# Moving x, sums and reciprocal transfers one step later in the first ten strips of an attention layer

## The chip, the cores and the metric

The kernel runs on one core of a Trainium2 chip. The metric is the device time of one execution in microseconds; the median of several executions is compared. The engines are TensorE (PE; its weight loads are shown as PEld), VectorE (DVE), ScalarE (ACT) and GpSimd (POOL). SyncE (SP) issues most of the transfers between the memory on the chip and HBM; GpSimd issues the indirect ones.

## The reference

The input x is 2 x 256 x 56 x 56. Two layers follow, each a mixer and a mixture of experts (MoE), both with a residual. Cut to its steps, with the weights left out:

```python
# layer 0: attention over a 7x7 window, 8 heads of 32, then 8 experts, the best two
x = x + attention(ln_c(x))              # q, k, v, o are 256x256; softmax over 49 neighbours
t = to_tokens(x)                        # 6272 tokens of 256
t = t + moe0(ln_t(t))                   # moe0(u) = u + sum over two experts of
x = from_tokens(t)                      #   weight * (gelu(u @ w1[e] + b1[e]) @ w2[e] + b2[e])
# layer 1: two ternary 3x3 convolutions with batch normalization, then 8 experts
x = x + conv(ln_c(x))                   # relu(o1 + bn(conv3x3(o1))), o1 = relu(bn(conv3x3(x)))
t = to_tokens(x)
t = t + moe1(ln_t(t))                   # hidden 512, the two largest probabilities as weights
```

The change lies in layer 0, between the attention's sums and the rows that are handed to the experts.

## The kernel before

**Strips.** The image is cut into 14 strips of 8 rows by 56 columns, seven to each of the two images. A strip has 448 tokens, held as four tiles of 112. The attention loop (L1577 to L1599) has one iteration for each strip g, and an iteration has eight steps: four column tiles by two halves of the channels. A step writes `scores` of its tile (q times k, L1435 and L1444, and the exponential, L1454) and `attend` of the step before: `av` on PE (L1464), added into `acc` by VectorE (L1474). `av` has two buffers. `acc` holds, for each pair of heads, the weighted values and, in further partitions, the sums of the exponentials. A step then advances `project(g + 2)` (the layer norm and q, k, v of a later strip) and calls `push`, which takes one step of every generator in `under_way`; a `yield` in such a generator therefore stands for one step of the loop.

**Leaving.** A strip can be finished once the strip below it has been attended to, as the windows overlap. So `leave(g - 1)` joins `under_way` at the end of iteration g; the last strip of an image follows with four steps' delay. `leave` (L1478 to L1548) does this:

- it loads x again and adds the output bias (`again`, L1319 and L1320);
- it writes the sums of the exponentials from `acc` to HBM (`sums`, L1491) and reads them back in another layout (`den`, L1496);
- it takes the reciprocal on VectorE (L1499), writes it to HBM (`shares`, L1500) and reads it back to the partitions of the heads (`rec`, two transfers, L1503); three small operations, `fit`, check the range of the sums (L1509 to L1511);
- it multiplies `acc` by `rec` into `oc` (eight operations of VectorE, L1520); for the first image `fresh` (L1354) then sets the strip's rows of `acc` for the second one;
- it multiplies by the output weights (`pw`, L1533) and adds to x (L1541);
- `norm0` normalizes the tokens (statistics on VectorE, the power on POOL at L713 to L715, the scaling on ScalarE at L721), transposes them (`pu`, L763; `ut`, L768), adds u to x on POOL (L770), stores x (`x_mid`, L771) and forms the gate's logits (`pl`, L777; the copy, L788). For strips 12 and 13 VectorE does what POOL does for the others.

For each pair of strips `settle0` then chooses two experts a token (L804 to L820, VectorE), ranks the rows (`rk` on PE) and scatters each row twice to its expert's place in HBM (16 indirect transfers of POOL, L860).

**The experts of layer 0.** The first 27 tiles of 128 rows or more are planned with the rows of the first ten strips alone (`FIRST`, L66): the plan is there when `counted0` is set by strip 9 (L832). In before the loop after the attention (L1601) pushes until the plan exists; by then it does. The remaining steps of `leave` and `settle0` for the last strips are taken one for each expert tile (`beside`), and when they are through, `routed_all` plans the later tiles. A tile has a load of its rows (`xg`, L1038), of its weights (`w`, L1049), transposes (`pt`, L1059), two products (`ph`, L1091; `py`, L1108) and a scatter of the result (L1118).

**Order.** Every engine, and every queue of transfers, executes in order what it has been given. An instruction that waits for a semaphore holds all behind it on its engine; for a transfer issued by SP that means all later transfers of SP. In the attention the order within each engine is set when the kernel is built, by a scheduler that works on the instructions as they are written down, so it doesn't always equal the written order. In the experts it is written out by hand for SP, VectorE, PE and ScalarE. Tile pools give out buffers in turn: `sums`, `shares`, `den` and `rden` have two each, `rec`, `oc` and `ut` one.

Of the kernel before, what the change touches and what calls it, by code (L numbers as in the profile page):

```python
# [10 lines left out]
F32 = mybir.dt.float32  # L11
# [4 lines left out]
ALU = mybir.AluOpType  # L16
# [22 lines left out]
LEAST, MOST = 1e-15, 1e15  # L39

E = 8
TT = NQ
# [22 lines left out]
DEN = HEADS * NT // TT  # L65
FIRST = (10, 10)  # L66
# [10 lines left out]
def bcast(ap, axis, shape):  # L77
    return ap.unsqueeze(axis).to_broadcast(shape)
# [551 lines left out]
def metaformer(ctx: ExitStack, tc: tile.TileContext, a: dict, out: bass.AP, flag):  # L630
    nc = tc.nc
# [87 lines left out]
    def scaled(dest, src, rstd, nmr):  # L719
        for t in range(NTT):  # L720
            nc.scalar.activation(  # L721
                dest[:, t, :],
                src[:, t, :],
                AF.Identity,
                bias=nmr[:, t : t + 1],
                scale=rstd[:, t : t + 1],
            )

    def routing(layer, wp, tp, ps):
# [18 lines left out]
        def norm(i, src, late=False):  # L748


            eng = nc.vector if late else small_eng
            rstd, nmr = yield from token_stats(tp, src, eps5, layer == 1 or late)
            row = rows[i] = tp.tile([TT, NTT, RW], F32, tag="u", name="u", bufs=U_BUFS[layer])
            u = row[:, :, :C]
            eng.memset(row[:, :, R_EX + 1 :], 0.0)
            eng.tensor_copy(row[:, :, R_ID], ids[:, i * NTT : (i + 1) * NTT])
            scaled(u, src, rstd, nmr)
            yield
            ut = tp.tile([P, KC, NT], F32, tag="ut", name="ut", bufs=1)
            for k in range(KC):  # L760
                pu = ps.tile([P, 512], F32, tag="aux", name="pu")
                for t in range(NTT):
                    nc.tensor.transpose(  # L763
                        pu[:, t * TT : (t + 1) * TT],
                        u[:, t, k * P : (k + 1) * P],
                        ident[:TT, :TT],
                    )
                nc.scalar.copy(ut[:, k, :], pu[:, :NT])  # L768
            if layer == 0:
                eng.tensor_tensor(src, src, u, ALU.add)  # L770
                nc.sync.dma_start(x_mid[i], src)  # L771
                yield
            lg = lgs[:, i * NTT : (i + 1) * NTT, :]
            pl = ps.tile([TT, NTT, E], F32, tag="pl" if layer else "aux", name="pl")
            for t in range(NTT):
                for k in range(KC):
                    nc.tensor.matmul(  # L777
                        pl[:, t, :],
                        ut[:, k, t * TT : (t + 1) * TT],
                        gate[:, k, :],  # L780
                        start=k == 0,
                        stop=k == KC - 1,
                    )
            if layer == 1:
                yield
                nc.vector.tensor_tensor(lg, pl, bcast(gate_b, 1, [TT, NTT, E]), ALU.add)
            else:
                nc.vector.tensor_copy(lg, pl)  # L788
            yield
# [400 lines left out]
    def blocks(ap):  # L1190

        return ap.rearrange("p h (t w) -> p t h w", w=TW)
# [100 lines left out]
    with ExitStack() as st:  # L1293
        aw = st.enter_context(tc.tile_pool(name="att_w", bufs=1, reuse_waits="tile"))
        tp = st.enter_context(tc.tile_pool(name="att_t", bufs=2, reuse_waits="tile"))
        ps = st.enter_context(tc.tile_pool(name="att_ps", bufs=2, space=PSUM, reuse_waits="tile"))
# [47 lines left out]
        fits = aw.tile([TT, DEN], F32, tag="fits", name="fits")  # L1344
# [15 lines left out]
            nc.gpsimd.memset(t[:, :, :, 1:3, :], 1.0)  # L1360
            vals.append(t)
        keys = {}
        norm0, settle0, tiles0, gates0, wgt0, counted0, _ = routing(0, aw, tp, ps)

        def project(g):
            s = g % NS
# [111 lines left out]
        def leave(g):  # L1478

            s = g % NS  # L1480
            rows = slice(s * SR, (s + 1) * SR)

            late = g >= len(STRIPS) - 2
            again(g, nc.vector if late else nc.gpsimd)


            sums = dram.tile([2, PAIRS * NT], F32, tag="sums", name="sums", bufs=2)
            shares = dram.tile([2, PAIRS * NT], F32, tag="shares", name="shares", bufs=2)
            den = tp.tile([TT, DEN], F32, tag="den", name="den")
            rden = tp.tile([TT, DEN], F32, tag="rden", name="rden")  # L1490
            for i in range(2):  # L1491
                nc.sync.dma_start(
                    sums[i : i + 1, :].rearrange("i (j h w) -> i j h w", h=SR, w=W),
                    acc[HD * (i + 1) : HD * (i + 1) + 1, :, rows, :],
                )
            nc.sync.dma_start(den, sums.rearrange("i (p n) -> (i p) n", n=DEN))  # L1496
            yield
            yield
            nc.vector.reciprocal(rden, den)  # L1499
            nc.sync.dma_start(shares.rearrange("i (p n) -> (i p) n", n=DEN), rden)  # L1500
            rec = tp.tile([P, PAIRS, NT], F32, tag="taken", name="rec", bufs=1)
            for i in range(2):
                nc.sync.dma_start(  # L1503
                    rec[3 * HD * i : 3 * HD * i + HD].rearrange("p j n -> p (j n)"),
                    shares[i].partition_broadcast(HD),
                )

            fit = tp.tile([TT, DEN], F32, tag="fit", name="fit")
            nc.vector.tensor_scalar(fit, den, LEAST, None, ALU.is_ge)  # L1509
            nc.vector.scalar_tensor_tensor(fit, den, MOST, fit, ALU.is_le, ALU.mult)  # L1510
            nc.vector.tensor_tensor(fits, fits, fit, ALU.add)  # L1511
            yield
            yield
            oc = tp.tile([P, KC, NT], F32, tag="oc", name="oc", bufs=1)
            for i in range(2):
                at = slice(3 * HD * i, 3 * HD * i + HD)
                for j in range(2):
                    to = HD * (2 * j + i)
                    for k in range(KC):
                        nc.vector.tensor_tensor(  # L1520
                            oc[to : to + HD, k, :].rearrange("p (t h w) -> p t h w", h=SR, w=TW),
                            blocks(acc[at, 2 * k + j, rows, :]),
                            blocks(rec[at, 2 * k + j, :].rearrange("p (h w) -> p h w", w=W)),
                            ALU.mult,
                        )
            if g < NS:
                fresh(s)
            yield
            for t in range(0, NTT, 2):
                pw = ps.tile([TT, 2, C], F32, tag="aux", name="pw")  # L1530
                for i in range(2):
                    for k in range(KC):
                        nc.tensor.matmul(  # L1533
                            pw[:, i, :],
                            oc[:, k, (t + i) * TT : (t + i + 1) * TT],
                            wt["o"][:, k, :],
                            start=k == 0,
                            stop=k == KC - 1,
                        )
                x = xr[g][:, t : t + 2, :]  # L1540
                nc.vector.tensor_tensor(x, pw, x, ALU.add)  # L1541
            yield
            yield from norm0(g, xr.pop(g), late)
            routed.append(g)
            if late:
                under_way.append(settle0([g]))
            elif g ^ 1 in routed:
                under_way.append(settle0([g & ~1, g | 1]))  # L1548
# [8 lines left out]
        def push():  # L1557

            for it in under_way[:]:
                if next(it, it) is it:  # L1560
                    under_way.remove(it)

        plans0, taken = [], []
# [34 lines left out]
                before = None  # L1598
                under_way.append(later(4, leave(g)))  # L1599
        loop.close()  # L1600
        while not plans0:  # L1601
            push()
            plan_first()

# [77 lines left out]
    with mid:  # L1682

        with ExitStack() as st:
            rp = st.enter_context(tc.tile_pool(name="raw", bufs=1, reuse_waits="tile"))
            tp = st.enter_context(tc.tile_pool(name="conv_t", bufs=2, reuse_waits="tile"))
            ps = st.enter_context(tc.tile_pool(name="conv_ps", bufs=4, space=PSUM, reuse_waits="tile"))
# [128 lines left out]
        with ExitStack() as both:  # L1816
# [6 lines left out]
            tp = both.enter_context(  # L1823
                tc.tile_pool(name="route_t1", bufs=2, side="right", reuse_waits="tile")
            )
            route_ps = ExitStack()
            ps = route_ps.enter_context(
                tc.tile_pool(name="route_ps1", bufs=2, space=PSUM, reuse_waits="tile")
            )
# [32 lines left out]
            norm, settle, tiles, gates, wgt1, _, sent = routing(1, wp, tp, ps)  # L1862
# [66 lines left out]
    with ExitStack() as st:  # L1929
        tp = st.enter_context(tc.tile_pool(name="last_t", bufs=2, reuse_waits="tile"))  # L1930
        ps = st.enter_context(tc.tile_pool(name="last_ps", bufs=2, space=PSUM, reuse_waits="tile"))
# [128 lines left out]
```

## Time and profile before

| | us |
|---|---|
| median of three runs | 1919.27 |
| lowest and highest run | 1911.3, 1926.04 |
| profiled execution, its time | 1925.16 |
| its span in the profile | 1923.3 |
| PE busy (share of the span) | 1564.4 (81%) |
| VectorE busy | 927.7 (48%) |
| ScalarE busy | 711.4 (37%) |
| POOL busy | 668.5 (35%) |

The mean clock that was granted to PE is 0.866. By stretches of the span the busy times are:

| stretch, us | what | PE busy | DVE | ACT | POOL | clock |
|---|---|---|---|---|---|---|
| 0 to 100 | loads, first strips | 82.2 | 47.0 | 41.6 | 40.2 | 1.00 |
| 100 to 569 | attention | 390.3 | 251.0 | 168.0 | 155.2 | 0.87 |
| 569 to 890 | experts of layer 0 | 262.4 | 175.2 | 124.2 | 153.7 | 0.90 |
| 890 to 1300 | convolutions | 338.3 | 273.7 | 178.3 | 146.9 | 0.88 |
| 1300 to 1470 | second routing | 84.7 | 84.4 | 47.7 | 90.4 | 0.52 |
| 1470 to 1923 | experts of layer 1, output | 406.5 | 101.8 | 153.0 | 103.5 | 0.92 |

A busy time is the time in which the engine executes something other than branches and waits, so a stretch of an engine that is not busy is either without work or waiting. A line such as L1533 is that of the kernel before; the release of a wait is inferred from semaphore events. "SPq" is SyncE as the issuer of transfers. In the views of waits the last three columns are the total, the number and the longest.

### The profile page before, as it was taken

The numbers are of one execution on the slowest core, as the hardware profiler recorded it, in microseconds if no ns is written. First come the engines' busy times: TensorE is split into PE (matmuls) and PEld (weight loads), VectorE is DVE, ScalarE is ACT, GpSimd is POOL, SyncE is SP. The second block draws the span as 40 slices with busy tenths as digits, with TensorE's granted clock in tenths as the row PEclk, the third lists the DMA queues.
The fourth block names the chain that finished last, engine by engine and source line by source line (L and its number), as shares of the span: only waits on it lengthen the run. The fifth ranks groups of instructions, "written<-read, shape, count | busy, mean of one in ns | idle before, by whom it ended". The sixth has DMA issues, their size and how long they took to land.

```text
span 1923.3 us, 26006 instructions
## 1 busy us (share of the span) xinstructions
PE 1564.4 (81%) x8709; PEld 1224.5 (64%) x8709; DVE 927.7 (48%) x2621; ACT 711.4 (37%) x1388; POOL 668.5 (35%) x676
## 2 busy tenths in 40 slices
PE   6999787797868875995789899966447999999964
PEld 3555454454537764784678788855335888888852
DVE  4467355354644425884787555575533111111136
ACT  3454332342323423542655352244223333333312
POOL 3013433414133564443355234235554222222210
PEclk9999798897968987997899999955557999999975
DMA  7032233212136676786653000033363787878758
GB/s 235 21 90 77 89 101 96 73 44 69 31 109 217 214 245 231 262 291 196 170 153 101 0 1 1 1 103 105 92 200 111 250 278 264 270 271 275 273 170 289
DMA packets 91887, 291.79 MB, mean 152 GB/s; under 512 B 20487, under 2 KB 35803, under 8 KB 80416
## 3 DMA queue, kind: packets, MB, share of 16 engines
q1 hardware_dynamic: 66736, 231.79, 38.3%
q0 software_dynamic: 21200, 51.82, 7.7%
q10 hardware_dynamic: 3808, 6.42, 1.0%
q8 instruction: 71, 1.16, 0.2%
q14 instruction: 72, 0.59, 0.1%
HBM read 218.51 MB, written 74.20 MB: 152 GB/s over the span
## 4 chain that ended last, share of the span: by engine, by line
PE 60%; DVE 14%; DMA 8%; issue 7%; another core or an unknown queue 6%; ACT 3%; POOL 2%; SPq 1%; DVEq 0%; POOLq 0%; ACTq 0%
PE ph L1091 13%; PE py L1108 12%; PE pc L1753 10%; PE av L1464 5%; PE pj L1387 4%; PE sc L1435 3%; DMA got<-ys 3%; PE pw L1533 3%; PE pv L1409 2%; PE pt L1059 2%; PE pl L777 2%; DVE t_stats L700 1%; DMA x_on<-x_mid 1%; PE pu L763 1%
## 5 line engine op out<-in xcount | busy, mean ns | idle before, releaser
L1091 PE MATMUL ph<-ut,w 128*128 128x256 f32 (+1 forms) x1472 | 317.6, 367 | 12.5 <-issue 6.5
L1108 PE MATMUL py<-w,h 128*128 128x256 f32 x1288 | 299.9, 381 | 2.4 <-issue 2.4
L1116 DVE TENSOR_TENSOR y<-py,w 128x512 f32<-128x512 f32 (+1 forms) x120 | 76.8, 640 | 441.7 <-PE py L1108 388.2
L1091 PEld LDWEIGHTS ph<-ut,w 128*128 128x128 f32 x1472 | 255.7, 198 | 43.9 <-issue 8.7
L860 POOL DMA_INDIRECT xs<-u,pos x224 | 213.7, 954 | 162.6 <-issue 97.7
L1753 PE MATMUL pc<-hi,wq 128*128 128x448 f32 x672 | 255.4, 381 | 16.6 <-ACT hi L1724 16.6
L1108 PEld LDWEIGHTS py<-w,h 128*128 128x128 f32 x1288 | 245.3, 192 | 36.0 <-issue 2.8
L1753 PE MATMUL pc<-lo,wq 128*128 128x448 f32 x672 | 254.1, 379 | 0.0
L1118 POOL DMA_INDIRECT ys<-y,dest x136 | 136.2, 1002 | 272.1 <-DVE dest L1066 186.4
L1098 ACT ACTIVATE h<-ph,w 128x256 f32<-128x256 f32 (+1 forms) x368 | 162.2, 448 | 129.0 <-PE ph L1091 74.1
L1454 ACT ACTIVATE ex<-sc 112x476 f32<-112x476 f32 (+3 forms) x224 | 116.7, 570 | 245.7 <-PE sc L1444 166.2
L1063 ACT COPY ut<-pt 128x512 f32<-128x512 f32 (+1 forms) x120 | 65.2, 543 | 308.3 <-PE pt L1059 246.0
L1474 DVE TENSOR_TENSOR acc<-av,acc 128x238 f32<-128x238 f32 (+3 forms) x224 | 87.6, 407 | 154.1 <-PE av L1464 72.4
L1464 PE MATMUL av<-ex,vals 112*64 112x238 f32 (+3 forms) x896 | 130.7, 413 | 28.6 <-DVE acc L1474 21.8
L1723 POOL TENSOR_TENSOR v<-pad 128x928 f32<-128x928 f32 (+1 forms) x56 | 98.3, 1761 | 159.4 <-DVE lo L1725 146.7
L1753 PEld LDWEIGHTS pc<-hi,wq 128*128 128x128 f32 x672 | 128.5, 192 | 31.8 <-ACT hi L1724 17.9
L1753 PEld LDWEIGHTS pc<-lo,wq 128*128 128x128 f32 x672 | 128.7, 192 | 15.4 <-DVE lo L1725 1.0
L1118 POOL DMA_INDIRECT ys<-y,to x81 | 84.4, 1042 | 127.3 <-DVE dest L1066 65.8
L1435 PE MATMUL sc<-q_im,keys 32*112 32x238 f32 (+3 forms) x896 | 99.3, 439 | 32.5 <-ACT ex L1454 21.2
L1464 PEld LDWEIGHTS av<-ex,vals 112*64 112x64 f32 x896 | 57.4, 146 | 83.5 <-issue 37.9
L713 POOL TENSOR_TENSOR t_rstd<-t_mv,eps 112x4 f32<-112x4 f32 x26 | 5.3, 203 | 280.9 <-DVE t_mv L702 280.9
L1724 ACT CAST hi<-v 128x928 fp32r<-128x928 f32 x56 | 54.1, 966 | 109.7 <-PE pc L1753 103.9
(237 smaller groups left out, 2286.1 us busy)
## 6 DMA issues: line engine op xcount, KB each, us to landing
w<-in_L_experts SPq DMA_DIRECT2D x64, 1154.0 KB
w<-in_L_experts SPq DMA_DIRECT2D x56, 641.0 KB
xg<-xs SPq DMA_DIRECT2D x97, 260.0 KB
got<-ys SPq DMA_DIRECT2D x28, 896.0 KB
acc<-in_fresh SPq DMA_DIRECT2D x14, 896.0 KB
xt<-in_x_tok SPq DMA_DIRECT2D x14, 448.0 KB
xr<-in_x_tok SPq DMA_DIRECT2D x14, 448.0 KB
rec<-shares SPq DMA_DIRECT2D x28, 224.0 KB
```

The lines of the kernel that those rows point to most:

```text
L860: w = nc.gpsimd.indirect_dma_start(xs[:, :], bass.IndirectOffsetOnAxis(ap=pos[:, j, t0 + t : t0 + t + 1], axis=0), us[t // NTT][:, t % NTT ...
L1091: nc.tensor.matmul(ph[:, :g], w1[:, k, f * P : (f + 1) * P], d["ut"][:, k, :g], start=k == 0, stop=k == KC - 1,)
L1098: nc.scalar.activation(d["h"][:, f, :g], ph[:, :g], AF.Gelu, bias=b1[:, f : f + 1])
L1108: nc.tensor.matmul(py[:, i, :], d["h"][:, f, i * P : (i + 1) * P], w2[:, f, :], start=f == 0, stop=f == NF - 1,)
L1118: o = nc.gpsimd.indirect_dma_start(ys[:, :], bass.IndirectOffsetOnAxis(ap=d["to"][:, i : i + 1], axis=0), y[:, i, :], None, bounds_check=T ...
L1387: nc.tensor.matmul(pj[:, :NT], wt[n][:, k, o * P : (o + 1) * P], xc[:, k, :], start=k == 0, stop=k == KC - 1,)
L1435: nc.tensor.matmul(sc[h // 2][:, h % 2, :nq], keys[g][p, c, tx * TT : (tx + 1) * TT], q_im[p, c, r0:r1, c0:c1], start=True, stop=False,)
L1454: nc.scalar.activation(e[:, :, :nq], sc[j][:, :, :nq], AF.Exp, scale=HD**-0.5)
L1464: nc.tensor.matmul(av[VW * i : VW * (i + 1), :nq], vals[g % 3][:, tx, 2 * c + j, 2 * i : 2 * i + 2, :].rearrange("p a d -> p (a d)"), ex[j ...
L1474: nc.vector.tensor_tensor(d, av[:, :nq].rearrange("p (h w) -> p h w", w=c1 - c0), d, ALU.add)
L1723: (nc.gpsimd if u else nc.vector).tensor_tensor(v[:, :, at : at + n, :], *r, op)
L1753: nc.tensor.matmul(pc[:, :NT], wq[:, k, c, dx * C + o * P : dx * C + (o + 1) * P], part[:, k, :, dx : dx + W], start=m == 0, stop=m == 2 * ...
```

## The change

Five things are moved. The number of a line is that of before.

1. In `norm0` the store of x to `x_mid` (L771) is written one step after the addition that produces it, instead of in the same step; this holds for all 14 strips.
2. In `leave`, for strips 0 to 9 (`calm`), one step more passes before the transfers of the sums (L1491 and L1496).
3. For the same strips one step more passes between the reciprocal (L1499) and the transfers of its result (L1500, L1503). The three operations of `fit` are written directly behind the reciprocal for all strips.
4. `fresh` is written a step later, together with the output product rather than with `oc`.
5. The loop after the attention pushes until the rows of strip 9 have been scattered (`sent0`), instead of until the plan exists.

```diff
--- before.py
+++ after.py
@@ -768,8 +768,8 @@
                 nc.scalar.copy(ut[:, k, :], pu[:, :NT])
             if layer == 0:
                 eng.tensor_tensor(src, src, u, ALU.add)
+                yield
                 nc.sync.dma_start(x_mid[i], src)
-                yield
             lg = lgs[:, i * NTT : (i + 1) * NTT, :]
             pl = ps.tile([TT, NTT, E], F32, tag="pl" if layer else "aux", name="pl")
             for t in range(NTT):
@@ -1360,7 +1360,7 @@
             nc.gpsimd.memset(t[:, :, :, 1:3, :], 1.0)
             vals.append(t)
         keys = {}
-        norm0, settle0, tiles0, gates0, wgt0, counted0, _ = routing(0, aw, tp, ps)
+        norm0, settle0, tiles0, gates0, wgt0, counted0, sent0 = routing(0, aw, tp, ps)
 
         def project(g):
             s = g % NS
@@ -1488,6 +1488,10 @@
             shares = dram.tile([2, PAIRS * NT], F32, tag="shares", name="shares", bufs=2)
             den = tp.tile([TT, DEN], F32, tag="den", name="den")
             rden = tp.tile([TT, DEN], F32, tag="rden", name="rden")
+
+            calm = g < FIRST[0]
+            if calm:
+                yield
             for i in range(2):
                 nc.sync.dma_start(
                     sums[i : i + 1, :].rearrange("i (j h w) -> i j h w", h=SR, w=W),
@@ -1497,6 +1501,13 @@
             yield
             yield
             nc.vector.reciprocal(rden, den)
+
+            fit = tp.tile([TT, DEN], F32, tag="fit", name="fit")
+            nc.vector.tensor_scalar(fit, den, LEAST, None, ALU.is_ge)
+            nc.vector.scalar_tensor_tensor(fit, den, MOST, fit, ALU.is_le, ALU.mult)
+            nc.vector.tensor_tensor(fits, fits, fit, ALU.add)
+            if calm:
+                yield
             nc.sync.dma_start(shares.rearrange("i (p n) -> (i p) n", n=DEN), rden)
             rec = tp.tile([P, PAIRS, NT], F32, tag="taken", name="rec", bufs=1)
             for i in range(2):
@@ -1504,11 +1515,6 @@
                     rec[3 * HD * i : 3 * HD * i + HD].rearrange("p j n -> p (j n)"),
                     shares[i].partition_broadcast(HD),
                 )
-
-            fit = tp.tile([TT, DEN], F32, tag="fit", name="fit")
-            nc.vector.tensor_scalar(fit, den, LEAST, None, ALU.is_ge)
-            nc.vector.scalar_tensor_tensor(fit, den, MOST, fit, ALU.is_le, ALU.mult)
-            nc.vector.tensor_tensor(fits, fits, fit, ALU.add)
             yield
             yield
             oc = tp.tile([P, KC, NT], F32, tag="oc", name="oc", bufs=1)
@@ -1523,9 +1529,9 @@
                             blocks(rec[at, 2 * k + j, :].rearrange("p (h w) -> p h w", w=W)),
                             ALU.mult,
                         )
+            yield
             if g < NS:
                 fresh(s)
-            yield
             for t in range(0, NTT, 2):
                 pw = ps.tile([TT, 2, C], F32, tag="aux", name="pw")
                 for i in range(2):
@@ -1598,7 +1604,7 @@
                 before = None
                 under_way.append(later(4, leave(g)))
         loop.close()
-        while not plans0:
+        while FIRST[0] - 1 not in sent0:
             push()
             plan_first()
```

## The prediction

> **What bounds the kernel now.** I first read the page's busy shares and its chain that ended last: PE is busy for 81% of the span and holds 60% of the chain. Then the waits of the DMA queue of SyncE, since the change moves what that queue is given (columns: who waits, for whom, us in total, times, longest).
>
> ```profile
> SPq L771 <- POOL xr L770: 82.7, 12, 11.3
> SPq L771 <- DVE xr L1541: 82.1, 10, 16.8
> ...
> SPq L1500 <- DVE fit L1509: 58.3, 7, 16.0
> SPq L1500 <- DVE fit L1510: 41.5, 5, 19.4
> ```
>
> So in the first 640 us SP stands some 165 us at the x_mid store and 114 us at the shares transfer (58.3 + 41.5 and 14.3 behind L1499), each time for an engine that has not yet delivered, with later loads queued behind it. That is a lot, but idle time of SP costs only what PE loses by it. The waits of PE in 0 to 600 us say how much:
>
> ```profile
> PE av L1464 <- DVE acc L1474: 21.8, 13, 3.0
> PE sc L1435 <- ACT ex L1454: 21.2, 7, 6.3
> ...
> PE pw L1533 <- DVE q_im L1399: 2.9, 2, 2.2
> PE pw L1533 <- DVE oc L1520: 2.9, 2, 2.4
> PE pt L1059 <- DMA xg<-xs: 2.5, 1, 2.5
> ```
>
> No line here names a load of the attention. What SP's lateness costs reaches PE through VectorE: DVE waits at oc for `rec`, and acc is queued behind oc. DVE's waits in 100 to 569 us:
>
> ```profile
> DVE acc L1474 <- remote: 49.9, 5, 15.3
> ...
> DVE oc L1520 <- DMA rec<-shares: 13.6, 7, 3.6
> ```
>
> The chain of waits, pieces from 0 to 700 us (start, length, what), shows one such place:
>
> ```profile
> 252.55 1.42 DMA shares<-rden
> ...
> 253.98 3.18 DMA rec<-shares
> ...
> 257.19 1.15 DVE oc L1520 x2
> ...
> 263.33 5.39 PE pw L1533 x16
> ```
>
> After the idle 2.22 us ahead of 263.33 the granted clock halves; columns: stretch, its length, busy PE, PE load, DVE, ACT, POOL, clock, DMA share, GB/s:
>
> ```profile
> 259.00:263.40 4.40, 2.18 (x18) 0.85 (x16) 4.31 (x9) 0.85 (x2) 0.00 (x0) 1.00 0.00 0
> 263.40:266.80 3.40, 3.40 (x8) 2.50 (x9) 2.06 (x9) 0.00 (x0) 1.18 (x2) 0.50 0.80 264
> 266.80:270.00 3.20, 3.20 (x17) 2.14 (x16) 2.87 (x10) 0.00 (x0) 0.23 (x2) 1.00 0.04 11
> ```
>
> A short gap thus costs its length and half of the 3.4 us at clock 0.50 that follow. Idle time and halved clock on PE are the path; all else below is judged by them.
>
> **The change part by part.** All sums are against the profiled execution's own 1925.16 us (span 1923.3, 1.9 around it), which lies 5.9 above the median of the runs, 1919.27.
>
> **A, rec and oc.** For strips 0 to 9 the sums, shares and rec transfers are issued one step later, and in the built order the reciprocal lies at most strips one step later on DVE too. Stalls that belong to a late rec in before: gaps ahead of pw of 2.22 (at 261.11), 2.41 (312.21) and 0.67 (438.27), gaps at av behind oc of 2.16 (327.55) and 2.95 (517.44): 10.4 us. Halved clock followed at 263.4 and 314.6 for 3.4 us each and at 519.4 for 6.8 us: 13.6 us, half of it lost, 6.8. Full worth 17.2 us. SP is freed of part of its waiting, but the distance from reciprocal to oc shrinks to one step: a steady strip takes 32 us in 8 steps, so 4.0 us, while shares and rec need 1.42 + 3.18 = 4.6. DVE then waits some 0.6 us, which two av buffers can cover. I take -11, the gaps without their clock; bounds -17 to +25 (worked out under the second rival).
>
> **B, the routing of a pair of strips.** Its DVE chain (L804 to L820, one piece of 1.67 us at L805 in the chain at 508.92, others of 0.24) stood ahead of acc five times: gaps of 1.59, 1.86, 1.76, 1.30 and 2.03 us at 165.97, 249.14, 343.40, 427.51 and 511.37, 8.5 us, with 3.4 us of halved clock behind two of them (another 3.4 us lost), 11.9 in all. In the built order of after the chain is split by oc, q_im or statistics for three of five pairs. I take half the gaps, -4; bounds -12 to 0.
>
> **C, the scatters.** POOL issues five trains of 16 indirect scatters (0.94 + 0.30 us each, some 20 us: 273.7 to 295.6, for one). PE loses 7 to 13 us of gaps in each, from about 6 us after the start until the end, some 53 us altogether, ended by what the profile calls remote (the 49.9 us above). I do not know why. In after each train is two steps later and is split by the residual add of L770 (2.36 us) as 2+14, 5+11, 16, 2+14, 16 where before it was 16, 4+12, 16, 16, 3+13. Nothing says that a train shrinks; what shifts is which matmuls it meets. I take -2, bounds -10 to +10, one train's gaps either way.
>
> **D, the start of the experts.** Before leaves the attention as soon as the plan is there; after pushes three steps more, until strip 9's rows are sent. Before's end of the attention, in the chain of waits:
>
> ```profile
> 567.28 1.53 PE av L1464 x8
> ...
> 572.38 5.39 DMA xg<-xs
> 577.77 0.04 issue
> 577.82 1.13 PE pt L1059 x4
> ```
>
> pw of strip 11 ends at 575.3 in before, and pt runs 2.5 us later. In after's built order pu and pl of strip 11 stand ahead of the first pt on PE, and on SP the xg loads stand behind x_mid of strip 11 and shares of strip 12, whose reciprocal stands on DVE behind the copy of pl (L788). By durations of these rows: pw 575.3, residual and statistics on DVE +1.9, L713 to L715 on POOL +1.6, u on ACT +2.5, pu +0.4 to its first half, ut +1.1, pl +1.9 (16 matmuls with their pipeline), lgs and reciprocal +0.6, shares' issue +0.4: 585.7. Some 1.1 us to the first xg issue, then 5.39 less the overlap of issue and landing: pt at about 591 in place of 577.8, 13.5 us. Of that, pu (0.93) and pl (1.65) are work that before did later among the experts: -2.6. I take +11; +6 if reciprocal and POOL's add are early, +16 if the clock is halved for one stretch more. The plan of the later rows comes two tiles sooner, which saves nothing, since its block of 20 us (gaps of 7.61 and 12.37 at 724.10 and 731.88) is as long.
>
> A rule of the Trainium skill bears here: by "TensorE: Matmul & The Clock Gate", section "What's actually happening", the array falls to half pulses after an idle window of about 3.4 us and is released after as long a busy one. The rows above disagree: 2.22 us of idleness was enough for 3.40 us at 0.50. By that page A could be worth only its 10.4 us of gaps, by the rows 17.2; and at D it speaks against the change, as the longer idle stretch would certainly be throttled (an estimate from that page: 1.7 us for one window more).
>
> **E, strip 12 among the experts.** In before SP stands at shares of strip 12 until 601.59, so the next xg goes at 604.57 and the next w at 605.94; PE waits 2.00 us at 606.04 and 2.55 at 609.02, and the clock stays near 0.5 for 6.8 us from 608.04. In after these shares are sent ahead of the xg loads. Full worth 4.55 + 3.4 = 8; I take -4, bounds -8 to 0, since strip 13 can stall in its place.
>
> **At nothing:** fit behind the reciprocal (three instructions, 0.03 us of chain between rden and shares in before), fresh one step later (needed only by acc of the second image, a strip's period away; uncovered it would cost one load, some 3 us, at most seven times), x_mid one step later. x_mid has a price of its own: the next xr load waits for it to land (21.9 us in 8 waits of SP), but xr is wanted only at L1541, ten steps on.
>
> Sum: -11 - 4 - 2 + 11 - 4 = -10, 1915 against the profiled execution, 1909 against the median; I take 1912.
>
> **The rivals.**
>
> *First, the stalls go entirely* (A and B with their clock, E, part of C): -17 - 12 - 8 - 5 + 11 = -31, 1894 or 1888, say 1891. For it: SP's 165 us at x_mid vanish almost wholly. Against: rec's distance of one step. It would show as no gap ahead of any pw.
>
> *Second, slower: rec comes too late at every strip.* The place is oc on DVE, with acc queued behind it and av behind acc with two buffers. It decides once rec lands later than 4.0 us behind the reciprocal by more than those buffers cover, which 4.6 us plus any wait of SP can do. Price: 0.6 us and more of gap and 1.7 us of halved clock, some 2.5 us a strip, ten strips: +25 in place of A's -11. With B, C, D, E as above: +26, 1951 or 1945, say 1946. Against it: before had oc waiting seven times for 13.6 us and PE lost only part.
>
> *Third, nothing happens in the attention:* each queue is served in order and the built SP order is nearly that of before (sums of the next strip ahead of x_mid, little else). Then D and E alone: +7, 1926.
>
> **How the numbers follow.** Forecast 0.35, first 0.28, second 0.22, third 0.15. About 1% is what a measurement of this kernel can tell from no change: under 1900 counts as faster, over 1938.5 as slower. Forecast and third rival lie between: faster 0.28, same 0.50, slower 0.22. The range reaches over most of the first and the second rival, 1888 to 1944; the likeliest's own is 1900 to 1926.
>
> **What would show it.** A right: no idle time ahead of pw at 255 to 320, SP's waits at L771 far under 165 us. A wrong: "oc <- rec" over 13.6 us. B: fewer gaps at acc behind L805. C: five trains, gaps within them still near 53 us; a change of over 10 would sink my sum. D: the first pt of the experts some 11 us later measured from the last av, with pu and pl before it. E: no gap at the fourth and fifth expert tile. I would be wrong above all where the trains of C change their size, since I have no cause for them, or where D's chain is longer than reckoned.

## The result and the profile after

The changed kernel takes 1940.33 us (median of three runs, 1940.15 to 1947.3) against 1919.27: a ratio of 1.0104, 95% interval 1.0065 to 1.0143. It is slower by 1%, where a gain of 0.4% was forecast. A second comparison, in the third set of runs below, gave 1.0106 (1.0060 to 1.0153). The profiled execution has a span of 1938.5 us, 15.2 more than before.

The waits of SP's queue in 0 to 640 us are what the change set out to alter. The line numbers of after are higher behind L770 (x_mid is L772, shares L1511, pw L1539):

```profile
SPq L1496 <- DVE acc L1474: 141.7, 8, 36.8
...
SPq L772 <- POOL xr L770: 59.5, 12, 8.2
...
SPq L1511 <- DVE fit L1507: 18.0, 8, 6.3
```

SP's waits at x_mid fell from 165 to about 63 us (59.5, and 3.9 behind L1547) and those at shares from 114 to some 42; it now stands at the sums instead. VectorE's waits in 100 to 580 us show that rec is not late any more, and that the scatters' "remote" is still there:

```profile
DVE acc L1474 <- remote: 61.2, 6, 15.7
...
DVE oc L1526 <- DMA rec<-shares: 4.8, 4, 1.7
```

But PE's waits in 0 to 600 us have only changed their name:

```profile
PE sc L1435 <- ACT ex L1454: 30.8, 12, 6.3
PE pl L777 <- ACT keys L1395: 19.0, 3, 9.9
...
PE av L1464 <- DVE acc L1474: 6.2, 8, 1.6
...
PE pw L1539 <- DVE oc L1526: 0.5, 1, 0.5
```

av behind acc fell from 21.8 to 6.2, pw's waits from 5.8 to under 1. In their place stand scores that wait for an exponential: twelve waits, 30.8 us. Before had 21.2 us of such waits, but nearly all in or at the scatters, 2.0 us outside them. Of the twelve, seven lie outside the scatters, 2.39, 2.39, 2.75, 2.03, 3.32, 2.45 and 2.45 us long, one for a strip, each about 7 us behind that strip's pw; an eighth, 2.10 us, lies at the start of a train. The place at strip 1, on ScalarE and PE (timeline: start, busy time, instruction, in brackets the idle time before it and what ended it):

```profile
159.68 1.03 ACT L1454 ACTIVATE ex<-sc 112x476 f32<-112x476 f32 x2 [6.00 <-PE sc L1444]
162.30 2.07 ACT L721 ACTIVATE u<-xr,t_nmr,t_rstd 112x256 f32<-112x256 f32 x4 [1.59 <-POOL t_nmr L715]
164.28 1.00 ACT L1454 ACTIVATE ex<-sc 112x476 f32<-112x476 f32 x2
```
```profile
161.46 1.02 PE L1464 MATMUL av<-ex,vals 112*64 112x238 f32 x8
164.88 1.73 PE L1435 MATMUL sc<-q_im,keys 32*112 32x280 f32 x8 [2.39 <-ACT ex L1454]
```

ScalarE takes up u, waits 1.59 us for POOL's statistics and scales for 2.07 us; the exponential that frees the scores' buffers stands behind it. Both were there in before:

```profile
147.90 1.03 ACT L1454 ACTIVATE ex<-sc 112x476 f32<-112x476 f32 x2 [7.30 <-PE sc L1444]
150.51 2.07 ACT L721 ACTIVATE u<-xr,t_nmr,t_rstd 112x256 f32<-112x256 f32 x4 [1.59 <-POOL t_nmr L715]
152.49 1.00 ACT L1454 ACTIVATE ex<-sc 112x476 f32<-112x476 f32 x2
```
```profile
148.84 1.98 PE L1409 MATMUL pv<-wv,xc 128*112 128x256 f32 x8
...
151.46 1.02 PE L1464 MATMUL av<-ex,vals 112*64 112x238 f32 x8
152.41 1.98 PE L1409 MATMUL pv<-wv,xc 128*112 128x256 f32 x8
```

The same hold of 3.66 us cost nothing there, as PE had a pv of the projection, 1.98 us, in each of the two steps. The built order of PE over a strip, from pw on (name and number of matmuls, runs of the same name together), shows the difference:

```
before    pw8 sc8 av4 pv4 sc8 av4 pv4 sc8 av4 sc8 av4 pu8 sc8 av4 pl8 sc8 av4 px8 sc8 av4 pj4 sc8 av4 pj4
after     pw8 sc8 av4 sc8 av4 sc8 av4 sc8 av4 px8 sc1 pu8 sc7 av4 pj4 pl8 sc8 av4 pj4 sc8 av4 pv4 sc8 av4 pv4
```

Of the eight steps of a strip three have no projection. Two steps more move pw from the sixth to the eighth step, and what follows it into those bare steps. Behind the new gap the clock is halved for 6.8 us; behind all seven it is halved for 37.6 us, of which half, 18.8 us, is lost (columns as in the prediction: stretch, length, busy times, clock, DMA share, GB/s):

```profile
162.48:164.88 2.40, 0.01 (x2) 0.01 (x1) 0.46 (x2) 2.40 (x6) 0.43 (x1) 0.79 0.02 6
163.90:170.70 6.80, 5.83 (x36) 3.05 (x38) 0.81 (x2) 3.08 (x7) 2.34 (x1) 0.50 0.24 72
```

The experts' start, in the chain of waits of after:

```profile
589.24 0.21 POOL t_nmr L715
...
589.48 1.10 ACT u L721 x2
...
592.68 3.23 PE pl L777 x16
...
596.04 0.34 DVE rden L1503
...
597.58 3.41 DMA xg<-xs
...
601.03 1.13 PE pt L1059 x4
```

The last av ends at 580.4 us (before 568.8), the first transpose starts at 601.0 (577.8): 20.7 us behind it instead of 9.0.

From here on "gaps outside the scatters" are PE's gaps between matmuls from 90 us to the last av, without those that begin in a train of scatters or within 3 us after it.

### The profile page after: what moved, and what is told of

The parts are those of the page before. It is cut to its first block, busy times and chain, and to the rows that moved or that the text cites. A ratio compares the mean times of both kernels' runs of the same rounds, so it can differ in the third digit from the quotient of the medians.

```text
span 1938.5 us, 26006 instructions
## 1 busy us (share of the span) xinstructions
PE 1572.1 (81%) x8709; PEld 1228.0 (63%) x8709; DVE 917.0 (47%) x2621; ACT 713.1 (37%) x1388; POOL 668.1 (34%) x676
## 4 chain that ended last, share of the span: by engine, by line
PE 61%; DVE 13%; another core or an unknown queue 7%; DMA 6%; issue 6%; ACT 4%; POOL 2%; SPq 0%; DVEq 0%; POOLq 0%; ACTq 0%
PE ph L1091 13%; PE py L1108 12%; PE pc L1759 11%; PE av L1464 5%; PE pj L1387 4%; PE sc L1435 4%; DMA got<-ys 3%; PE pl L777 2%; PE pv L1409 2%; PE pt L1059 2%; PE pw L1539 2%; DVE t_stats L700 2%; PE pu L763 1%; DVE oc L1526 1%
## 5 line engine op out<-in xcount | busy, mean ns | idle before, releaser
L1091 PE MATMUL ph<-ut,w 128*128 128x256 f32 (+1 forms) x1472 | 313.3, 364 | 6.9 <-issue 4.4
L1759 PEld LDWEIGHTS pc<-hi,wq 128*128 128x128 f32 x672 | 128.4, 191 | 31.7 <-ACT hi L1730 17.8
L1464 PE MATMUL av<-ex,vals 112*64 112x238 f32 (+3 forms) x896 | 135.6, 428 | 8.3 <-DVE acc L1474 6.2
L1435 PE MATMUL sc<-q_im,keys 32*112 32x238 f32 (+3 forms) x896 | 106.8, 464 | 41.3 <-ACT ex L1454 30.8
L1435 PEld LDWEIGHTS sc<-q_im,keys 32*112 32x112 f32 x896 | 47.8, 191 | 86.5 <-ACT ex L1454 51.4
L777 PE MATMUL pl<-gate,ut 128*112 128x8 f32 x448 | 71.8, 292 | 36.7 <-ACT keys L1395 19.0
```

The costliest lines, as they stand in the source:

```text
L777: nc.tensor.matmul(pl[:, t, :], ut[:, k, t * TT : (t + 1) * TT], gate[:, k, :], start=k == 0, stop=k == KC - 1,)
L1091: nc.tensor.matmul(ph[:, :g], w1[:, k, f * P : (f + 1) * P], d["ut"][:, k, :g], start=k == 0, stop=k == KC - 1,)
L1435: nc.tensor.matmul(sc[h // 2][:, h % 2, :nq], keys[g][p, c, tx * TT : (tx + 1) * TT], q_im[p, c, r0:r1, c0:c1], start=True, stop=False,)
L1464: nc.tensor.matmul(av[VW * i : VW * (i + 1), :nq], vals[g % 3][:, tx, 2 * c + j, 2 * i : 2 * i + 2, :].rearrange("p a d -> p (a d)"), ex[j ...
L1759: nc.tensor.matmul(pc[:, :NT], wq[:, k, c, dx * C + o * P : dx * C + (o + 1) * P], part[:, k, :, dx : dx + W], start=m == 0, stop=m == 2 * ...
```

## The experiments

**First set: which part, and why.** Theory: the two steps alone move u into a step without projection, and the loop's steps delay the experts. All four run beside the kernel before, 1919.26 us.

*No extra steps* (x_mid, fit, fresh and the loop stay):

```diff
-            calm = g < FIRST[0]
-            if calm:
-                yield
...
-            if calm:
-                yield
```

> The changed kernel without its two extra steps in the leaving of strips 0 to 9; the moved x_mid, fresh, fit and the longer loop stay. Theory (the extra steps alone did it: they move the scaling of u on ScalarE from the last step of a strip, where the projection gives PE 1.98 us of pv, to the second step of the next strip, where it gives PE nothing): the built order of the attention is that of before, so the new waits of sc for ex (nine gaps of 2.0 to 3.3 us in the changed kernel) are gone, the last av ends near 569, and the time is that of before, 1912 to 1928. Rival (x_mid, fit or fresh carry the loss): the gaps stay and the time stays above 1933.

1927.56 us (ratio 1.0034, 1.0012 to 1.0055). The built order of the attention is that of before on every engine, the last av ends at 571.0, the waits named are gone (2.2 us at sc behind ex are left outside the scatters, as in before). So x_mid, fresh and fit as such moved nothing in the attention: what is written a step later is put back where its inputs are ready. The loop still pushes once; the first transpose comes 12.2 us behind the last av instead of 9.0. The time is 8.3 us over before, and beyond these 3.2 us no cause of it was found.

*u on VectorE:*

```diff
-            scaled(u, src, rstd, nmr)
+            if layer == 0 and i < FIRST[0]:
+                for t in range(NTT):
+                    nc.vector.tensor_scalar(u[:, t, :], src[:, t, :], rstd[:, t : t + 1],
+                                            nmr[:, t : t + 1], ALU.mult, ALU.add)
+            else:
+                scaled(u, src, rstd, nmr)
```

> The changed kernel with the scaling of u (four operations) on VectorE instead of ScalarE for strips 0 to 9; all else as changed. Theory: ScalarE is no longer held for 2.07 us ahead of the exponential, so the gaps of PE at sc waiting for ex outside the scatters fall from 17.8 to under 5 us, the halved clock behind them goes too, the last av ends at 558 to 568 instead of 580, and the time falls from 1940 to 1917 to 1928. Rival (the late output product costs whichever engine scales, through VectorE and acc): gaps appear at av waiting for acc instead, the last av stays at 576 or later, the time at 1935 or more.

1950.96 us, slower still (1.0162, 1.0132 to 1.0191), with the last av at 589.2: the rival's outcome. VectorE now stands at u for POOL, with acc behind it (timeline of VectorE and PE, then PE's waits in 90 to 569 us):

```profile
161.09 0.74 DVE L759 TENSOR_SCALAR u<-xr,t_rstd,t_nmr 112x256 f32<-112x256 f32 x2 [1.48 <-POOL t_nmr L715]
161.74 0.71 DVE L1485 TENSOR_TENSOR acc<-av,acc 128x238 f32<-128x238 f32 x2
162.19 1.02 PE L1475 MATMUL av<-ex,vals 112*64 112x238 f32 x8 [1.87 <-DVE acc L1485]
```
```profile
PE av L1475 <- DVE acc L1485: 28.4, 17, 3.8
```

So it is the wait for POOL, in whatever engine's order u stands, as much as the 2.07 us of ScalarE.

*Six extra steps instead of two:*

```diff
             calm = g < FIRST[0]
             if calm:
-                yield
+                for _ in range(5):
+                    yield
```

> The changed kernel with six extra steps instead of two for strips 0 to 9 (five before the sums, one before the shares), so that in the built order u stands in the sixth step of a strip, beside 3.27 us of projection on PE. Theory: what counts is the work of the step and not the lateness, so the gaps of sc behind ex fall under 5 us outside the scatters and the last av ends at 560 to 572. The loop behind the attention gets longer by up to four steps, so the first experts' transposes come later than 20 us after the last av, and the total is anywhere from 1925 to 1950. Rival (lateness itself costs): gaps as in the changed kernel or more, last av at 580 or later, 1945 or more.

1916.54 us (0.9988, 0.9971 to 1.0004): later still, and 24 us faster than the changed kernel. The time is under the expected range. The gaps at sc behind ex outside the scatters are 5.5 us in three waits, just over the limit set. The last av ends at 544.9, earlier than expected: more work is put off past it, and the gaps in the scatters are 36.7 us here instead of the 55.6 of before, for a reason that was not found. The first transpose then comes 44.1 us behind the last av. So lateness as such does not make the gaps at sc.

*The loop alone:*

```diff
+        for _ in range(3):
+            push()
```

> The kernel before, with three more steps of the leaving strips between the attention and the experts: the loop's part of the change alone. Theory (steps written ahead of the experts stand in order ahead of their loads on SP and their transposes on PE): the first transpose of the experts comes 9 to 14 us later than in before (there 577.8, 9.0 behind the last av), with pu and pl ahead of it; half or more of it is given back by the end of the experts; time +2 to +7, 1921 to 1927. Rival (in the changed kernel the late start came from the later steps of strip 11, not from the loop): the first transpose moves by less than 4 us and the time by less than 2.

The first transpose comes 21.6 us behind the last av instead of 9.0, 12.6 us as expected. The time, 1932.49 (1.0063, 1.0037 to 1.0089), rose by 13, twice the upper end of what was expected: by this the start was not given back.

**Second set: the projection moved, and shorter loops.** The kernel before took 1780.09 us here, 140 less, so its numbers are set beside one another only. The last section says what differed.

*The projection two steps later:*

```diff
-            ahead = project(g + 2) if g + 2 < len(STRIPS) else iter(())
+            ahead = later(2, project(g + 2)) if g + 2 < len(STRIPS) else iter(())
...
+                    next(behind, None)
                     next(ahead, None)
...
-            finish(ahead)
+            finish(behind)
+            behind = ahead
```

> The changed kernel with the projection of strip g + 2 started two steps later in its iteration, its last two steps (the pv products) running over into the first two steps of the next one; the leaving strips are as late as in the changed kernel, and the loop is as long. Theory (the loss is that u, with its wait for POOL, holds ScalarE's exponentials in a step in which PE has no projection): pv stands behind pw again as in before, so the gaps at sc behind ex fall from 17.8 to under 5 us outside the scatters, the last av ends at 555 to 568 instead of 580, and the start of the experts stays at 19 to 23 us behind it; time 1915 to 1930. Rival (lateness of the output product itself): gaps and last av as in the changed kernel within 5 us, 1935 or more.

The gaps at sc behind ex fell to 6.8 us in three waits, still over the theory's limit of 5: one of 3.95 us lies behind a u that waited 5.63 us for POOL. The time is 1800.8 (1.0123, 1.0082 to 1.0165), as the rival has it. With the projection the old stalls came back (PE's waits in 90 to 500 us):

```profile
PE av L1464 <- DVE acc L1474: 18.1, 12, 3.1
PE pw L1539 <- DVE q_im L1399: 10.5, 6, 3.3
```

It restored much of the pattern of before, stalls included, on top of the long loop (21.6 us). This experiment did not tell the theories apart.

*The same, with the two extra steps for strips 0 to 7 alone:*

```diff
-            calm = g < FIRST[0]
+            calm = g < FIRST[0] - 2
```

> The kernel of the projection two steps later, with the two extra steps for strips 0 to 7 alone, so that the loop behind the attention is short again. Theory (both losses gone, the gain of the earlier stalls kept): last av as there, 555 to 568, the first transpose of the experts 9 to 14 us behind it instead of 20, time 1905 to 1918, below before. Rival (the late start is owed to something else than the loop's steps): 19 us or more behind the last av, and a time within 4 us of the kernel with the full loop.

1802.35 us (1.0120, 1.0081 to 1.0159): the start is short, 11.7 us, but the last av came 12.0 us later. Of that 8.9 us had gathered by 406 us, up to where both kernels have the same order on every engine, so most of it is the chance of two executions: over the attention the granted clock lost 38.1 us here and 28.2 there. Why the medians are no lower either was not settled.

*Six extra steps for strips 0 to 7, four for strip 8, none for strip 9:*

```diff
-            calm = g < FIRST[0]
-            if calm:
+            calm = {FIRST[0] - 2: 4, FIRST[0] - 1: 0}.get(g, 6 if g < FIRST[0] else 0)
+            for _ in range(calm - 1):
                 yield
```

> The changed kernel with six extra steps for strips 0 to 7, four for strip 8 and none for strip 9, the projection where it was: u falls into the step of 3.27 us of pj, and the loop is short. Theory: gaps at sc behind ex under 5 us outside the scatters, last av 550 to 563, first transpose 9 to 14 us behind it, time 1902 to 1916, faster than six extra steps for all ten strips (1916.5). Rival (the short time with six steps came from work put off past the attention): last av at 565 or later, time 1917 or more.

1787.15 us (1.0035, 1.0009 to 1.0061). Gaps (4.7 us) and start (12.5 us) are as the theory expects, yet no gain on before came of them here, and why is open. With the pace of this set neither the expected times nor the rival's can be read.

*The step behind the reciprocal alone:*

```diff
             calm = g < FIRST[0]
-            if calm:
-                yield
```

> The changed kernel with one of its two extra steps, that between the reciprocal and the transfers of its result. u then stands in the first step of a strip, which has no projection on PE either. Theory: the gaps at sc behind ex are there as in the changed kernel, 13 to 24 us of them outside the scatters, last av 574 to 584, time 1930 to 1941. Rival (each extra step costs its own half, through the lateness): gaps of about half, 7 to 11 us, last av near 576, time 1926 to 1932.

1780.34 us (1.0014, 0.9992 to 1.0037), and 8.4 us of gaps in nine waits: the rival's size, with a ratio under that of its times. The built order explains the gap at strip 1. One of the two pv now stands behind pw, as PE's timeline at strip 1 shows:

```profile
153.68 1.98 PE L1409 MATMUL pv<-wv,xc 128*112 128x256 f32 x8
...
158.07 0.91 PE L1435 MATMUL sc<-q_im,keys 32*112 32x238 f32 x6 [0.74 <-ACT ex L1454]
```

With two pv behind pw (before) the gap at this strip is nothing, with one 0.74, with none 2.39. So at this place it is not "bare or not" that counts but how much of the hold PE can fill: one pv of 1.98 us took 1.65 off the gap. The rival, that each step costs its own half, is not excluded by this run.

**Third set: u taken off the engines that PE waits for.** The kernel before took 1921.75 us. First come the two kernels themselves, unedited: before, and the changed one.

> The kernel before, unchanged, for a trace on the chip of this set of runs, as the last set ran some 140 us faster than the first. Both theories: the order of the instructions is the same, so the built-in stalls ahead of pw and acc are the same; if this chip is the faster one, the stalls inside the scatters of POOL (55.6 us of PE gaps in the first trace) are what is missing, with 15 us or less of them left.

This set ran at the pace of the first. The scatters held PE for 56.1 us of gaps (55.6 in the first trace), and the last av ended at 572.8.

> The changed kernel, unchanged, on the chip of this set. Theory (u with its wait for POOL holds the exponentials in a step without projection, and the loop delays the experts; neither needs the stalls of the scatters): gaps at sc behind ex of 15 us or more outside the scatters, the first transposes 19 to 23 us behind the last av, and the changed kernel slower than before by 0.6 to 1.5% on either chip. Rival (the loss depends on the scatters' stalls): on a chip without them it is within 0.4% of before.

1943.18 us, 1.0106. The seven gaps outside the scatters are 2.39, 2.39, 2.75, 2.03, 3.32, 2.46 and 2.45 us, those of the first trace to 0.01, so they belong to the order and not to chance (an eighth, of 0.34 us, has none beside it there); the first transpose comes 21.3 us behind the last av. As this set had the scatters' stalls, the rival about them was not tried.

*u on POOL*; against the edit with VectorE above:

```diff
-                    nc.vector.tensor_scalar(
+                    nc.gpsimd.tensor_scalar(
```

> The changed kernel with the scaling of u on POOL instead of ScalarE for strips 0 to 9, behind POOL's own statistics; the order on PE is nearly that of the changed kernel. Theory: neither ScalarE nor VectorE waits for POOL any more with exponentials or acc behind it, so the gaps at sc behind ex fall under 5 us outside the scatters without new ones at av behind acc, the last av ends 10 to 22 us earlier than in the changed kernel of this set, and the time is lower by 8 to 20 us. Rival (what costs is the bare steps of PE in themselves, whoever scales): last av and time within 5 us of the changed kernel.

1922.27 us (1.0000, 0.9978 to 1.0022), 20.9 below the changed kernel. No gap at sc behind ex is left outside the scatters, and the last av ends at 560.0 instead of 587.8. PE's order is that of the changed kernel, so its bare steps are not what costs. Timeline of POOL and ScalarE at strip 1:

```profile
157.55 0.20 POOL L715 TENSOR_TENSOR t_nmr<-t_nmr,t_rstd 112x4 f32<-112x4 f32 x1
157.86 2.17 POOL L759 TENSOR_SCALAR u<-xr,t_rstd,t_nmr 112x256 f32<-112x256 f32 x4
```
```profile
157.03 1.03 ACT L1465 ACTIVATE ex<-sc 112x476 f32<-112x476 f32 x2 [0.84 <-PE sc L1455]
158.98 1.17 ACT L1465 ACTIVATE ex<-sc 112x560 f32<-112x560 f32 x2 [0.92 <-PE sc L1455]
```

POOL scales in 2.17 us right behind its own statistics, and the exponentials follow the scores within 0.9 us.

PE's idle time hardly shrank, though. From 90 us to the last av it is 74.3 us in the changed kernel and 72.3 here: 18.1 us at sc behind ex went, but outside the scatters the gaps at av behind acc rose from 7.0 to 12.9 us, which the theory had excluded, and the gaps in the scatters rose from 47.5 to 54.4. What came down is the time at half clock (the changed kernel, then this one; the clock is the third number from the end):

```profile
90.00:587.79 497.79, 423.42 (x2826) 246.88 (x2822) 247.00 (x744) 173.35 (x336) 155.09 (x181) 0.84 0.24 71
```
```profile
90.00:560.01 470.01, 397.05 (x2819) 233.98 (x2817) 248.49 (x741) 152.67 (x294) 178.43 (x221) 0.89 0.26 76
```

By its unrounded records the clock lost 78.5 and 49.5 us in these two stretches. The difference of 29.0 us is as large as the 27.8 us by which the last av is earlier. Some of it is chance, as the first trace of the changed kernel lost 70.0 us. So the gain came less from shorter gaps than from clock: the gaps that took the place of those at sc were followed by less halved clock.

*u on POOL, and the two extra steps for strips 0 to 7 alone:*

```diff
-            calm = g < FIRST[0]
+            calm = g < FIRST[0] - 2
```

> The kernel with u on POOL, with the two extra steps for strips 0 to 7 alone: the loop behind the attention is short, 9 to 14 us from the last av to the first transpose instead of 19 to 23. Theory: last av as with u on POOL (within 5 us), and the time lower than there by 3 to 12 us, below before by 0.2 to 1%. Rival (what the late start costs is given back among the experts anyway): the time within 3 us of the kernel with u on POOL.

1908.51 us, 0.9925 of before (0.9897 to 0.9953): faster than both kernels. The first transpose comes 12.5 us behind the last av instead of 22.0. The last av itself ends 7.7 us earlier, at 552.3, more than the 5 us expected; the gaps in the scatters are 42.9 us instead of 54.4. So the gain is not that of the loop alone.

## Why the prediction was wrong

The third set divides the change, by medians: from before to the short loop with u on POOL -13.2 us, the steps of strips 8 and 9 with the long loop +13.8, u back on ScalarE +20.9: together +21.4. The loop alone, on before, gave +13.2. The first of the three also holds whatever u on POOL is worth in before, which was not tried; as the gaps at sc behind ex outside the scatters are 2.0 us in before, little can come from these.

**The step that failed** is the first sentence of A: the later steps were followed for the transfers, the reciprocal and oc, and priced where VectorE and SP stand. That pw takes everything behind it along by two steps, the scaling on ScalarE among it, was not followed to the step where it lands, and neither A nor "at nothing" has a term for it. "A steady strip takes 32 us in 8 steps, so 4.0 us" treated the steps as alike; three of them have no projection. The missing term is 17.8 us of gaps outside the scatters and the 18.8 us lost to halved clock behind them. As the old stalls went at the same time, the loss by the granted clock outside the scatters rose by 14.8 us only, from 24.8 in before to 39.6. By the run with u on POOL it cost 21 us of the median, which by itself turns -10 into +11. The other 10 us up to the measured +21 lie in the terms that were there: A, B, C and E were taken at -21 and the third set has -13 for them and for u on POOL together, and D was taken at 11 and cost 13.8.

**A was right, in direction.** Gaps ahead of pw fell from 5.3 to 0.4 us, of those at av behind oc one of 1.56 is left, and oc's waits for rec fell from 13.6 to 4.8 us. So the second rival, which ended on this side at 1946, is not what happened: near its time, by another mechanism. That a wait at rec costs only what PE loses shows in the kernel with u on POOL: there oc waits 30.5 us for rec in seven waits, more than in before, and of PE's gaps only 1.1 us at pw and some 2.2 at av (318.55, behind an oc that waited 1.69) lie behind them.

**B was right.** Gaps of av behind VectorE's acc fell to a few of about 0.8 us or less and one of 0.99 outside the scatters, beside the one behind oc. **C came out near its value,** without a cause and so by luck: 55.6 us of gaps in the trains became 52.5, in the second pair of traces 56.1 became 47.5. **E was right:** the gaps of 2.00 and 2.55 us at the fourth and fifth tile are gone, one of 0.91 stands in their place.

**D was right in mechanism and size at its place**, 11.7 us for 11, along the chain that was written down: from the end of pw to the first transpose 15.1 us (585.94 to 601.03), for 15.7. The median lost 13 to 14 us by it. In the first pair of traces the whole lag shrank from 23.2 us at the first transpose to 14.0 at the last py of these experts, in the second pair it grew from 27.0 to 31.4, so what is given back is no fixed part of it.

**Third rival:** for the moves of x_mid, fit and fresh it is what happened; the built order didn't change by them.

Of the 11.6 us by which the last av is later, the terms give 6.8: gaps +2.2 outside the scatters and -3.1 in them, clock +14.8 and -7.1. The other 4.8 were not found.

## What to carry to other kernels

When an operation is put off by a step, follow every engine that it and its followers use to the place where they land, and ask there what the engine on the path has to do meanwhile: a wait that was free beside other work costs its length, and here half clock behind it, where that work is missing. An operation that waits for a slow engine belongs on that engine, or on one that nobody urgent queues behind. And steps pushed through ahead of a stage with an order of its own were paid here at that stage's first load.

## What the runs showed of the hardware

The same order need not give the same clock. In before the gap of 2.16 us at 327.55 left the clock at full; in three other executions with that order, the repeated before, the one with three more steps and the one with no extra steps, a gap of 2.15 us at the same place was followed by 10.2 us at half (the stretch of 10 us behind it, in before and in the repetition):

```profile
330.00:340.00 10.00, 10.00 (x80) 7.01 (x76) 7.54 (x22) 2.75 (x6) 3.77 (x4) 1.00 0.51 157
```
```profile
330.00:340.00 10.00, 10.00 (x34) 6.57 (x32) 4.65 (x11) 1.06 (x2) 2.34 (x1) 0.55 0.48 154
```

By the Trainium skill's "TensorE: Matmul & The Clock Gate", section "What's actually happening", the gate looks at windows that run free of the kernel. That fits a gap that is sometimes punished and sometimes not, and it fits the trace of before, in which the halved stretches of 263.41, 283.89, 314.61 and 345.33 us start 6, 9 and 9 times 3.41 us apart. The section ties the half clock to an idle window of about 3.4 us; here gaps of 2.03 to 3.32 us were enough. At this one place 5.1 us hang on it. How much of the spread of the runs of before (1911 to 1931) comes from such places was not measured.

In the second set PE's gaps in the five trains of scatters were 4.8 to 15.3 us in all instead of 37 to 57, VectorE showed no wait for "remote" in the attention, and the same kernel before was 140 us faster. The trains took as long as ever (20.1 to 22.1 us for the first; 19.9 to 22.1 in the other sets). So the scatters' instructions by themselves are not what holds PE; what does was not found. Their gaps are also not all of the 140 us: the attention of the kernel with the step behind the reciprocal alone ended 62 us before that of the first trace, and the rest lies behind it. The changed kernel was not run there.
